# A dilated GraphSAGE behind masked attention: output parts of two batches held until each batch norm, the last products in all eight PSUM banks, and tiles of the first loads given other homes

## The chip, the cores and the metric

The kernel runs on one core of one Trainium2 chip. The metric is the device time of one execution in microseconds (us), the median of a few runs. The profile is one more execution, recorded by the hardware profiler. Its spans are named by engine: PE (TensorE matmul), PEld (its weight load), DVE (VectorE), ACT (ScalarE), POOL (GpSimd) and SP (SyncE, which here only issues DMAs).

## The reference, cut to what matters

Sixteen graphs (b) of 1024 nodes and 128 features go through two residual layers. The first is attention with eight heads, masked and weighted by the adjacency matrix. The second first thins the adjacency row by row ("dilation"), and then runs three SAGE convolutions, each with a batch norm over all graphs and nodes:

```python
h = jnp.maximum(_layernorm(x), 0.0)
x = x + attention(h, adj, ...)                  # mask adj == 0, softmax, times adj
h = jnp.maximum(_layernorm(x), 0.0)
adj_d = _dilate(adj, mask)                      # sequential in the rows of each graph
def _sage(x, adj, Wr, Wx, b, mf):
    agg = einsum('bij,bjd->bid', adj, x) / deg
    out = agg @ Wr + x @ Wx + b
    return out / maximum(norm(out), 1e-12) * mf[..., None]
def _bn(x, g, b):
    m, v = mean(x, axis=(0, 1)), var(x, axis=(0, 1))
    return (x - m) * rsqrt(v + 1e-5) * g + b
h1 = _bn(relu(_sage(h,  adj_d, Wr1, Wx1, b1, mf)), g1, be1)
h2 = _bn(relu(_sage(h1, adj_d, Wr2, Wx2, b2, mf)), g2, be2)
h3 = _bn(relu(_sage(h2, adj_d, Wr3, Wx3, b3, mf)), g3, be3)
x = x + (concatenate([h1, h2, h3]) * mf @ Wl + bl) * mf
```

Each batch norm needs the whole of its layer before anything of the next layer can start.

## The kernel before, in words

Everything is in one function, `swept` (L35); `walked` (L1327) is a fallback behind a flag and is not taken here.

**First part, 0 to about 2370 us.** `attention()` (L462) goes over `turns` of (graph b, half c of 512 nodes, block m of 128 nodes). A turn has two halves g of four heads. For each half PE makes scores in `scores` (L521): sixteen 32x32 matmuls add minus infinity where there is no edge (L536, from `nomask`), four products of keys and queries follow (L542). ACT takes the exponential (L579), DVE multiplies by the adjacency (L584), PE sums (`values`, L466). `turn_over` (L479) makes a turn's transposed adjacency: PE transposes (L487), ACT copies (L490) and makes `nomask` (L494), and six DMAs on SP's queue copy `nomask` onto itself at other partitions (L498, L499). `prepare(b)` (L282) makes keys, queries and values; its layer norm ends in a power on POOL (L272). `dilation()` (L621) runs beside attention; for its first block it reads 16 adjacency rows tiles of 512 KB (L650, POOL's queue). `biases()` (L90) splits five bias vectors in three bf16 pieces. `node_masks()` (L227) makes the mask columns.

**The three SAGE layers, about 2370 to 3498 us.** A turn is (layer L, graph b, half c), about 10 us. `nodes` (L1083) is a generator: PE makes the node's own part (L1094) and 4 x 16 aggregation products (L1108, "sums"); then, one turn later and between the next turn's sums, "scaled" (DVE L1126, ACT square L1131), "norm" (DVE L1134 to ACT L1137), "result" (DVE L1139 to L1141), "transposed" (PE L1145, ACT copy into `hTs` L1146) and "end" (DVE statistics, L1148). DVE also masks the next turn's adjacency (L142). `given` (L1074) makes the next graph's products with Wr, `incoming` (L1066) applies the batch norm to a graph on ACT (L1072). `output_part(L-1, b, h, ...)` (L1018) is what a layer adds to the output: four matmuls (L1023) and four DVE adds into `prev` (L1030), with a store to DRAM after the second half. It runs beside the turn c = 1 of graph b, except for the last graph, whose two parts come after the layer.

**After each layer** (L1281 to L1294): the last half's stages without anything beside them, the matmuls of the last graph's parts, the aggregate of the statistics (L1285), the square root on ACT (L1288), four small DVE steps to the scale and shift (`affine`, L1289 to L1292), then the DVE adds of the parts. Then ACT applies `affine` to the next layer's graph 0.

**The last products, about 3498 us to the end.** For each graph `come` (L1305) applies the batch norm on ACT (two instructions), `output_part(2, ...)` makes two halves in three PSUM banks in turn ("y", "n", "o", L1317). Half 0 takes four DVE adds. In half 1 DVE adds two blocks, ACT multiplies the other two (L1038) and DVE adds those in one step (L1039). SP stores each half to `out` (L1041).

**What sets the order.** PE, ACT and DVE keep the order in which the Python code calls them (`manual_schedule`, L1183). SP and POOL issue in an order that the framework chooses by when a tile's buffer is free. A tile belongs to a tag of its pool with so many buffers, and a new tile waits until the tag's oldest tile is no longer read. A DMA also waits for the one issued eight before it on the same kind of queue. Readers of one PSUM tile on different engines are put one after the other, in the order of the code.

## Time and profile before

| | us |
|---|---|
| median of 3 runs (3560.0 to 3562.39) | 3561.78 |
| the profiled execution | 3556.3 |
| its span, first to last instruction | 3554.4 |
| PE busy | 3445.8 (97%) |
| DVE busy | 3174.0 (89%) |
| ACT busy | 2290.9 (64%) |
| start of the first exponential, L579 | 27.73 |
| end of `affine` of the three layers, L1292 | 2763.2, 3133.2, 3498.6 |
| end of the last DVE add, L1039 | 3547.2 |

Busy is a sum over instructions. The span also holds what comes before and behind them on their engines, and the execution has 1.9 us around the span. A row of the timeline gives the start in us, the busy time in us, engine, line, operation, output<-input with shapes, the count, and in brackets the idle time of that engine just before and what ended it. A row of stretches gives the busy time of each engine in it, the granted TensorE clock (PEclk, 1.00 is full), the mean busy share of the DMA engines and what they moved.

### The profile page before, as it was taken

The page shows a single profiled execution, that of the slowest core. Times are in us where ns is not written, and L with a number is a line of the kernel's source. Part 1 is how long each engine was busy: PE and PEld are TensorE (multiplying, and loading weights), DVE is VectorE, ACT ScalarE, POOL GpSimd, SP SyncE. Part 2 cuts the span into 40 slices and gives each one's busy share as a digit, 9 for nine tenths or more (in the row PEclk, how much of TensorE's full clock was granted, in tenths as well). Part 3 has the DMA queues.
Part 4 walks back from the last instruction along what each step waited for, and adds up shares of the span by engine and source line. Part 5 has one row for each costly group of instructions (what it writes and reads, how often), then busy time and mean ns, then how long its engine had stood idle before and what let it go on. Part 6 is the DMA issues. An engine that isn't in the chain of part 4 may idle for free.

```text
span 3554.4 us, 86070 instructions
## 1 busy us (share of the span) xinstructions
PE 3445.8 (97%) x34855; PEld 1893.8 (53%) x34855; DVE 3174.0 (89%) x5254; ACT 2290.9 (64%) x3781; POOL 179.0 (5%) x253
## 2 busy tenths in 40 slices
PE   8999999999999999999999999999999899999997
PEld 3333333333333333333333333338999899989996
DVE  7999999999989999999999999987878788878886
ACT  6699689679769869968976885873232333322224
POOL 2000000000000000000000000000000000000000
PEclk9999999999999999999999999999999999999999
DMA  7356356447537636735754763667999799989995
GB/s 231 102 169 201 123 159 199 142 135 214 168 111 222 195 116 201 227 111 170 235 157 133 235 205 110 209 213 285 331 331 326 266 328 328 329 295 333 333 332 184
DMA packets 650122, 772.27 MB, mean 217 GB/s; under 512 B 173264, under 2 KB 569168, under 8 KB 637424
## 3 DMA queue, kind: packets, MB, share of 16 engines
q1 hardware_dynamic: 632672, 708.58, 61.7%
q0 software_dynamic: 15456, 57.30, 4.9%
q8 instruction: 275, 4.51, 0.5%
q14 instruction: 135, 1.11, 0.1%
q10 hardware_dynamic: 1584, 0.79, 0.1%
HBM read 508.50 MB, written 157.29 MB: 187 GB/s over the span
## 4 chain that ended last, share of the span: by engine, by line
PE 48%; DVE 39%; ACT 6%; DMA 3%; issue 3%; SPq 1%; POOL 0%; ACTq 0%; DVEq 0%; POOLq 0%
DVE w L584 16%; PE pg L1108 16%; PE sc L542 6%; PE acc L469 5%; PE acc L474 5%; DVE wr L872 4%; PE pn L1079 2%; DVE hit L807 2%; ACT e L579 2%; PE sc L536 2%; PE own L1094 2%; PE py L1023 2%; DMA nomask<-nomask 1%; PE pt L1145 1%; DVE aT L142 1%
## 5 line engine op out<-in xcount | busy, mean ns | idle before, releaser
L584 DVE TENSOR_TENSOR w<-e,aT 128x1024 f32<-128x1024 f32 x1024 | 1204.2, 1217 | 91.2 <-ACT e L579 90.9
L579 ACT ACTIVATE e<-sc 128x1024 f32<-128x1024 f32 x1024 | 990.9, 1020 | 376.1 <-PE sc L542 375.0
L1108 PE MATMUL pg<-y,aT 128*128 128x128 f32 (+1 forms) x6144 | 738.0, 275 | 0.0
L1108 PEld LDWEIGHTS pg<-y,aT 128*128 128x128 f32 x6144 | 712.4, 192 | 0.0
L469 PE MATMUL acc<-w,v_both 128*32 128x512 f32 x4096 | 673.1, 607 | 8.6 <-DVE w L584 3.8
L474 PE MATMUL acc<-e,eps 128*32 128x512 f32 x4096 | 650.5, 596 | 0.0
L542 PE MATMUL sc<-qT,kT 32*128 32x512 f32 x4096 | 584.8, 641 | 0.0
L142 DVE SCALAR_TENSOR_TENSOR aT<-mr,aT 128x1024 f32<-128x1024 bf16 x384 | 458.9, 1217 | 0.0
L474 PEld LDWEIGHTS acc<-e,eps 128*32 128x32 f32 x4096 | 165.9, 110 | 295.1 <-issue 285.2
L1131 ACT ACTIVATE sq<-o 128x512 f32<-128x512 f32 x96 | 60.5, 631 | 363.4 <-DVE o L1126 363.4
L872 DVE TENSOR_TENSOR_SCAN wr<-rk 128x1024 f16<-128x1024 bf16 x128 | 291.7, 2279 | 0.0
L536 PEld LDWEIGHTS <-never 32*32 32x32 bf16 x8192 | 79.1, 88 | 345.3 <-issue 323.6
L536 PE MATMUL sc<-nomask,never 32*32 32x512 bf16 x8192 | 249.6, 385 | 12.5 <-ACT e L579 8.0
L469 PEld LDWEIGHTS acc<-w,v_both 128*32 128x32 f32 x4096 | 106.4, 108 | 233.9 <-DVE w L584 140.2
L542 PEld LDWEIGHTS sc<-qT,kT 32*128 32x128 f32 x4096 | 160.1, 183 | 116.6 <-issue 116.6
L487 PEld LDWEIGHTS pa<-ident,a 128*128 128x128 f32 x1024 | 108.2, 142 | 182.4 <-issue 143.5
L1146 ACT COPY hT<-pt 128x512 f32<-128x512 f32 x96 | 56.3, 587 | 224.2 <-PE pt L1145 223.2
L1126 DVE SCALAR_TENSOR_TENSOR o<-pg,rdeg,mine 128x128 f32<-128x128 f32 x384 | 108.1, 344 | 92.2 <-PE pg L1108 90.4
L885 ACT ACTIVATE wr<-wr,th 128x1024 f16<-128x1024 f16 x128 | 148.0, 1156 | 46.7 <-DVE wr L872 45.8
L487 PE MATMUL pa<-ident,a 128*128 128x128 f32 x1024 | 168.7, 288 | 7.0 <-DMA a<-in_adj 6.3
L494 ACT ACTIVATE nomask<-aT 128x512 bf16<-128x512 f32 x256 | 161.4, 630 | 8.1
L490 ACT COPY aT<-pa 128x512 f32<-128x512 f32 x256 | 151.6, 592 | 11.5 <-PE pa L487 6.8
(222 smaller groups left out, 3949.8 us busy)
## 6 DMA issues: line engine op xcount, KB each, us to landing
aT<-aT_d SPq DMA_DIRECT2D x94, 2048.0 KB, 9.0
mr<-mr_d SPq DMA_DIRECT2D x188, 512.0 KB, 5.8
aT_d<-aT SPq DMA_DIRECT2D x256, 256.0 KB, 4.0
a<-in_adj SPq DMA_DIRECT2D x253, 256.0 KB, 4.0
ad<-in_adj SPq DMA_DIRECT2D x112, 512.0 KB, 4.1
nomask<-nomask SPq DMA_DIRECT2D x512, 96.0 KB, 2.7
nomask<-nomask SPq DMA_DIRECT2D x512, 64.0 KB, 2.6
nomask<-nomask SPq DMA_DIRECT2D x512, 32.0 KB, 2.6
```

Of the source, the lines that this page charges most:

```text
L142: nc.vector.scalar_tensor_tensor(part, mrs[h][:, j : j + 2, :].rearrange("p j n -> p (j n)"), 0.0, part, ALU.is_equal, ALU.mult)
L469: nc.tensor.matmul(acc[g][32 * j : 32 * j + 32, :], v1[:, m, 2 * j + g, :], ws[j // 2][:, j % 2, :], start=(m == 0), stop=False,)
L474: nc.tensor.matmul(acc[g][32 * j : 32 * j + 32, :], eps8, es[j // 2][:, j % 2, :], start=False, stop=(m == NB - 1),)
L487: nc.tensor.transpose(pa[:, k * P : (k + 1) * P], a[:, k, :], ident)
L490: nc.scalar.copy(aT[:, 0, :], pa)
L494: nc.scalar.activation(nomask[:, 0, :], aT[:, 0, :], AF.Relu, bias=1.0, scale=-1e38, accum_out=zeros[:, i : i + 1])
L536: nc.tensor.matmul(scs[j // 2][to : to + 32, j % 2, :], never[rows, rows], nomask[rows, j, :], start=True, stop=False, tile_position=(32 * ...
L542: nc.tensor.matmul(scs[j // 2][:, j % 2, :], kT[rows, mm], qTs[c][rows, g, :], start=False, stop=True, tile_position=(32 * j, 0),)
L579: nc.scalar.activation(e, scs[q], AF.Exp, scale=1.0 / math.sqrt(HD))
L584: nc.vector.tensor_tensor(w, es[q], aT.to_broadcast([P, 2, HN]), ALU.mult)
L872: nc.vector.tensor_tensor_scan(wrs[b], rk(b, 1, N + 1), rk(b, 2, N + 2), -1023.0, ALU.add, ALU.add)
L1108: nc.tensor.matmul(pg[:, i // 2, at : at + width], aT[:, j, i * P : (i + 1) * P], y[:, j, :width], start=(j == 0), stop=(j == NB - 1),)
```

## The change

1. **First loads.** `biases()` starts ahead of the loads of x. Its three pieces become three tiles, one in tag "mr" and two in tag "xin", the home of the x tiles. The node mask and its float copy move to tag "ad", the home of the dilation's row tiles. `node_masks()` is called in the first half of turn 2 instead of turn 0. The six loads of the batch norm's weights (`norms`) move from a constant tile to a tile that is opened after the first part.
2. **Held parts.** In layers 1 and 2 the output parts of the last two graphs are held: the matmuls of graph 14 stand right behind the last half's "scaled", those of graph 15 behind its "end", in banks "o", "g", "g", "y" ("g" is half of a two-bank score tile). All 16 DVE adds come after `affine`.
3. **The step to `affine`.** For the last half of a layer the statistics are taken before ACT's copy. One small DVE step is put beside the square root, and one goes.
4. **Last products.** Each graph has two banks, in a rotation over all eight: two score tiles, then "t" and "n", then "o" and "y". PE makes both halves of a graph at once, `come` runs two graphs ahead, and the add of ACT's two blocks is made after the next graph's first four adds.

The parts of the diff that carry this:

```diff
         for i, name in enumerate(names):
             nc.gpsimd.dma_start(vecs[0][:, i, :], t[name].rearrange("(o d) -> o d", o=1))
+        pieces = [
+            shared.tile([1, n, D], BF, name=f"pieces{i}", tag="xin" if i else "mr", bufs=3 if i else 4)
+            for i in range(3)
+        ]
         yield
-        pieces = shared.tile([1, 3, n, D], BF, name="pieces", tag="mr", bufs=4)
...
+        bias_pieces = biases()
+        next(bias_pieces)
         load_x(0)
         for i in range(3):
             load(i, nc.scalar)
-        bias_pieces = biases()
-        next(bias_pieces)
...
-        nr_i = pool.tile([B * NB, P], I32, name="nr_i", tag="qT")
+        nr_i = shared.tile([B * NB, P], I32, name="nr_i", tag="ad", bufs=2)
...
                     elif g == 0:
+                        go_on_with(True)
+                    if (i, g) == (2, 0):
                         node_masks()
-                        go_on_with(True)
...
+        last_half = b == B - 1 and c == 1
+        if last_half:
+            nc.vector.bn_stats(late["stats"][:, 2 * b + c, :], pt)
         nc.scalar.copy(hTs[b][:, c * HN : (c + 1) * HN], pt)
         yield "transposed"
-        nc.vector.bn_stats(late["stats"][:, 2 * b + c, :], pt)
+        if not last_half:
+            nc.vector.bn_stats(late["stats"][:, 2 * b + c, :], pt)
...
+            held, last_parts = ["o", "g", "g", "y"], []
...
                     if c == 1 and L > 0:
-                        parts = [output_part(L - 1, b, h, hT, prev, "y" if more or h == 0 else "o") for h in range(2)]
-                        if more:
+                        at_end = b + 2 >= B
+                        parts = [output_part(L - 1, b, h, hT, prev, held.pop(0) if at_end else "y") for h in range(2)]
+                        if at_end:
+                            last_parts += parts
+                        else:
...
-            go(before, "scaled", "norm", "result", "transposed", "end")
-            for part in parts:
+            go(before, "scaled")
+            for part in last_parts[:2]:
                 next(part)
+            go(before, "norm", "result", "transposed", "end")
+            for part in last_parts[2:]:
+                next(part)
...
             nc.scalar.activation(mv[:, 1:2], mv[:, 1:2], AF.Sqrt, bias=bn_eps)
+            nc.vector.scalar_tensor_tensor(mv[:, 2:3], mv[:, 0:1], -1.0, late["norms"][:, L, 0:1], ALU.mult, ALU.mult)
             nc.vector.reciprocal(mv[:, 1:2], mv[:, 1:2])
-            nc.vector.tensor_tensor(affine[:, 0:1], norms[:, L, 0:1], mv[:, 1:2], ALU.mult)
-            nc.vector.tensor_tensor(mv[:, 0:1], mv[:, 0:1], affine[:, 0:1], ALU.mult)
-            nc.vector.tensor_tensor(affine[:, 1:2], norms[:, L, 1:2], mv[:, 0:1], ALU.subtract)
-            for part in parts:
+            nc.vector.tensor_tensor(affine[:, 0:1], late["norms"][:, L, 0:1], mv[:, 1:2], ALU.mult)
+            nc.vector.scalar_tensor_tensor(
+                affine[:, 1:2], mv[:, 2:3], mv[:, 1:2], late["norms"][:, L, 1:2], ALU.mult, ALU.add
+            )
+            for part in last_parts:
                 whole(part)
...
+        def products(b):
+            if b % 4 < 2:
+                both = ps_s.tile([P, 2, 512], F32, name=f"py_3_{b}", tag="sc")
+                pys = [both[:, c, :] for c in range(2)]
+            else:
+                pys = [bank(f"py_3_{b}_{c}", ("t", "n", "o", "y")[2 * (b % 2) + c]) for c in range(2)]
...
+        come(0)
+        come(1)
+        before = None
+        for b in range(B):
+            pys = products(b)
+            of = [pys[k // HB][:, (k % HB) * P : (k % HB + 1) * P] for k in range(NB)]
+            for k in range(HB):
+                add(b, k, of[k])
+            leave(b, 0)
+            if before:
+                finish(*before)
+            tmp = late["pool"].tile([P, NB - mine, D], F32, name=f"tmp_{b}", tag="mine")
+            for k in range(mine, NB):
+                nc.scalar.mul(tmp[:, k - mine, :], of[k], mf2[:, b * NB + k : b * NB + k + 1])
+            for k in range(HB, mine):
+                add(b, k, of[k])
+            come(b + 2)
+            before = b, tmp
+        finish(*before)
```

`add` is one DVE multiply-and-add of a 128x128 block, `finish` one DVE add of two blocks from `tmp` and the store of half 1, `leave` the store of a half (`mine` is 6).

## The prediction

> **What bounds the kernel now.** I read the page's chain that ended last first, then the places that the change touches in the timeline: the first 35 us, a layer's end, the tail. The chain's first lines:

> ```profile
> PE 48%; DVE 39%; ACT 6%; DMA 3%; issue 3%; SPq 1%; POOL 0%; ACTq 0%; DVEq 0%; POOLq 0%
> ```

> Most of the time goes along PE and DVE, in loops that are not touched. So the change can only work on dead time at three kinds of places. The start:

> ```profile
> 9.34 1.35 SPq L653 DMA_DIRECT2D ad<-in_adj  x1
> ...
> 10.32 1.06 POOL L272 TENSOR_TENSOR rs_a<-rs_a,minus_half 128x4 f32<-128x4 f32 x1
> ...
> 12.38 0.62 SPq L498 DMA_DIRECT2D nomask<-nomask  x1
> ...
> 24.42 1.25 PE L536 MATMUL sc<-nomask,never 32*32 32x512 bf16 x6 [0.32 <-DMA nomask<-nomask]
> ...
> 27.73 1.94 ACT L579 ACTIVATE e<-sc 128x1024 f32<-128x1024 f32 x2 [4.68 <-PE sc L542]
> ```

> POOL's power starts at 10.32, though DVE had its input ready at 7.92 (L271, 7.75 for 0.17): six loads of batch norm weights stand ahead of it. The first nomask copy is issued at 12.38, though ACT had the mask at 8.67: two x loads and two ad loads stand ahead on SP. PE waits for these copies until 24.42.

> The end of layer 2 (graph 15's last aggregate ends at 3124.2), with the clock in stretches of 1 us:

> ```profile
> 3128.55 1.09 PE L1145 MATMUL pt<-ident,o 128*128 128x128 f32 x4 [4.33 <-DVE o L1141]
> 3129.22 3.54 PEld L1023 LDWEIGHTS py<-weights,h 128*128 128x128 f32 x16
> ...
> 3130.30 0.70 DVE L1148 BATCH_NORM_STATS2 stats<-pt 128x6 f32<-128x512 f32 x1 [1.89 <-ACT hT L1146]
> ```
> ```profile
> 3126.00:3127.00 1.00, 0.00 (x0) 0.00 (x0) 0.82 (x2) 0.11 (x1) 0.00 (x0) 1.00 0.80 248
> 3127.00:3128.00 1.00, 0.00 (x0) 0.00 (x0) 0.66 (x4) 0.20 (x1) 0.00 (x0) 0.81 1.04 410
> 3128.00:3129.00 1.00, 0.45 (x2) 0.48 (x3) 0.41 (x1) 0.00 (x0) 0.00 (x0) 0.50 1.03 426
> ```

> PE sits idle 4.33 us, the granted clock halves, and the statistics wait for ACT's copy. The tail, one graph of sixteen:

> ```profile
> 3508.59 1.64 DVE L1030 SCALAR_TENSOR_TENSOR outs<-py,mf,outs 128x128 f32<-128x128 f32 x6
> ...
> 3510.32 0.63 ACT L1038 ACTIVATE tmp<-py,mf 128x128 f32<-128x128 f32 x2 [0.45 <-DVE outs L1030]
> 3510.97 0.43 DVE L1039 TENSOR_TENSOR outs<-outs,tmp 128x256 f32<-128x256 f32 x1 [0.75 <-ACT tmp L1038]
> ```

> DVE and ACT take turns: 1.64 + 0.09 + 0.63 + 0.02 + 0.35 to the next graph's adds make the period of 2.73 us.

> **The start: 5.5 us saved.** In the program of the change POOL's power waits for DVE alone: 7.95 in place of 10.32, so h follows at about 9.25, not 11.61. PE is just done with the weights' transposes by then (10.03). The chain h, hT, pa, aT, pk, pq keeps its lengths (11.61 to 20.04, less 2.36), so q is written by ACT at 17.7 to 19.2. On SP the x loads now wait for the pieces' copies and the ad loads for the node mask, so they stand behind. The first nomask copy can go at about 8.9, the sixth at about 12. With 2.6 us to land (page, copies' median) to 5.4 (the same in the first 75 us) all are there at 15 to 17.5, before PE is done with pq (17.7). Then 16 mask matmuls (1.7, from four in 0.43) and 2.09 for L542: the first exponential at 21.5 in place of 27.73, 6.2 us. What is late next: ACT, which from 30.6 on is busy without a gap; it simply runs ahead by that much.

> What this costs: xt 1 is issued only when a_4 and the bias copies have landed (6 to 6.9 us by the DMA view), about 20.3, and lands at about 26. Its statistics on DVE are due then, behind the first w, and the next w waits for an exponential that ends at 28, so I book 0; without that cover it is 1 us. `node_masks` in turn 2 puts 0.22 on DVE, a PE transpose behind the sums of the previous turn and 0.8 on DVE behind that, about 1.7 with the wait, ahead of w at 47.06; but DVE next waited 1.60 there for an ad load (51.09). Booked 0.2; at turn 0 it had cost 0.6, which goes. The stretch 40 to 60 moves 335 to 348 GB/s with the DMA engines full; one of the two ad loads (0.5 MB, 1.5 us) now falls into it: booked 0.7. So 6.2 - 0.7 = 5.5, ends 2.5 (DMA takes the lead back) and 6.7. The six weight loads, 0.55 each on POOL, go to about 2375, where POOL waits 3 to 5 us between issues and its next loads wait for PE anyway: 0.

> **The step to affine: 2.4 us.** At each of three layer ends the statistics no longer wait for ACT's copy (0.59 + 0.03), and the copy runs beside the aggregate (1.02): -0.62. One of four DVE steps of 0.195 goes, and the new one (0.16) fits into DVE's 0.36 wait for the square root: -0.19. Together 3 x 0.81. If readers were not put in this order it is 3 x 0.19.

> **Graph 14's parts: 3.6 us.** Beside its turn they take two times 0.89 us of PE (L1023 on the chain), with PE the bound. Now 16 matmuls run in the idle 4.33 us. PE then still comes to pt after DVE's o (6.1 against 5.3 us into the turn), so no wait opens: 2 x 1.8. No pg waits for a DMA in this stage, so the loads have slack; lower end 2 x 1.2. The eight adds (2.2 us of DVE) move behind `affine`, ahead of the masks of the next turn: these end at about 9 us after affine, and PE needs them at 16. Held banks are free after 1.1 to 4.4 us; own needs "o" at 5, pg at 5 to 8. Booked 0. The queue behind: POOL's store of graph 14 and load of the next `prev`, wanted 20 us later.

> **The clock: 3.7 us.** No row shows PE warm after a gap of about 2.3 us, so I bound it. From below: the three gaps of the page (clock down 3.3 to 5 us after the last matmul) with nothing gained if any gap cools it, 0. [...] pt takes 0.63 in place of 1.09 at both ends (2 x 0.46); parts of graph 15 fill the next gap; and layer 3's first products (3134.06 to 3141.22, 7.16 us, all at 0.50) take 1.06 + 0.67 + 1.06 + 0.3 + 1.1 = 4.2 and some issue: -2.8. By the rows alone the term is 0 to 3.7[...]. I take 3.7, since the rows do have drops only after 3.2 us. At layer 1's end PE stays idle 4.7 us, and nothing changes.

> **The tail: 6.5 us.** ACT's two blocks no longer stand between DVE's adds and DVE's last step. Graphs in two-bank tiles: ACT waits for four adds (1.10), then 0.09 + 0.63, 0.03, two adds 0.55, so 2.40, with `finish` (0.43) inside the wait. Graphs in single banks: ACT does not wait, and ACT's own 0.63 + 1.52 sets 2.15 to 2.2. The mean is 2.29, so 16 x 2.29 + 0.45 = 37.1. Ahead of it DVE now has 16 adds, 4.4 (3.3 from affine to the first out add before). So affine to last add is 41.5, against 3547.2 - 3498.6 = 48.7: 7.2. The first products wait for "g" (2.3 us after affine); at half clock 16 take 3.6 and DVE starts 1.5 later; I take half of that. SP waits for the loads of graphs 14 and 15 before most stores, until 8.5 us after affine (7.9 before), and 0.52 MB per 2.29 us is 229 GB/s, with the DMA engines at 0.69 for 205 now: just covered. Ends 4.5 and 7.3.

> Sum: 5.5 + 2.4 + 3.6 + 3.7 + 6.5 = 21.7. The profiled execution, 3556.3, would become 3534.6. The runs' median lies 5.5 above it; the same step gives 3540.

> **Rivals.**
> - Clock still drops: 3.7 and 0.7 of the tail go: 3544. For it: [...] after 4.3 us of work at half clock it stayed at half. Chance 0.22.
> - The loads lead again in 40 to 60 us: 3 us of the start go, 3543. For it: two waits of DVE for ad there, 4.2 in total. Chance 0.15.
> - The tail stays in lockstep or at the stores' rate (2.6 or more per graph): 3545. Against: no store is on the chain but one. Chance 0.08.
> - Slower: SP is held by x load 1, which waits for the bias copies. Behind it stand the masks of turn 2, needed by PE at about 37. They need 11 us, so a landing after 26 us costs one for one; a loss of 7 net of 21.7 needs it at 55. The slowest copy now lands at about 23.7. Chance 0.02.
> - The banks or homes do nothing at all (a place where another wait takes over each gain): within 0.2%, 0.03.
> - My forecast, 3540: 0.50.

> **How the numbers follow.** A measurement can tell about 0.2%, 7.1 us. All cases but the last two are faster: 0.95; same 0.03; slower 0.02. With all upper ends 24.6 and a spread of 2 it is 3535; with start 2.5, clock 0 and tail 4.5 together 3549, and 2 for the spread. I say 3534 to 3551.

> **What would show it.** First exponential near 21.5; first nomask copy near 9; statistics right behind pt; affine steps 0.58 apart in place of 0.77; PEclk 1.00 at pt and through layer 3's first products; tail period 2.2 to 2.4 with ACT nearly full; end of the last add 41 to 43 us after affine. Wrong if DVE or ACT waits for DMA between 25 and 60, if pt still takes 1.09, or if SP's stores lag behind DVE.

## The result, and the profile after

| | before | after |
|---|---|---|
| median of five runs, us | 3561.08 | 3540.96 |
| lowest and highest | 3558.74, 3562.39 | 3538.31, 3553.21 |
| the profiled execution | 3556.3 | 3540.29 |

The ratio of the runs is 0.995, with a 95% interval of 0.9932 to 0.9967: 20 us faster, known to some 6 us either way. The pair of profiled executions differs by 16.0 us only. That gap of four is itself a subject below, since everything that is read by stage comes from single traces. The layers are counted 1 to 3 here, as in the prediction (L = 0 to 2 in the code).

Where the two traces part, stage by stage (start times unless the row says end):

| | before | after | gained on the way here |
|---|---|---|---|
| first exponential | 27.73 | 20.14 | 7.6 |
| 65th product w (exponential times adjacency, DVE L584, L594 after) | 172.55 | 169.68 | -4.7 |
| first aggregate of layer 1 | 2417.26 | 2416.82 | -2.4 |
| affine of layer 2, end | 3133.16 | 3128.30 | 4.4 |
| first aggregate of layer 3 | 3141.22 | 3133.44 | 2.9 |
| affine of layer 3, end | 3498.61 | 3487.64 | 3.2 |
| last DVE add, end | 3547.25 | 3529.66 | 6.6 |
| end of the span | 3554.41 | 3538.50 | -1.7 |

The chain that ended last is of no use here. On the page of the profile after it holds nothing but the last DVE steps ("DVE 0%"); two of the last three stores have no landing in this trace, which is probably why it stops there. So the reading goes by place. The start, from the timeline of after (start, busy, engine, line, operation, tiles, count, and in brackets the idle time before with what ended it):

```profile
7.53 1.04 POOL L274 TENSOR_TENSOR rs_a<-rs_a,minus_half 128x4 f32<-128x4 f32 x1 [2.39 <-DVE rs_a L273]
...
9.07 0.62 SPq L507 DMA_DIRECT2D nomask<-nomask  x1
...
17.15 0.65 PE L545 MATMUL sc<-nomask,never 32*32 32x512 bf16 x16
...
20.14 1.92 ACT L589 ACTIVATE e<-sc 128x1024 f32<-128x1024 f32 x2
```

POOL's power waits for DVE alone and stands at 7.53, the first nomask copy at 9.07. All sixteen mask matmuls run in one piece of 0.65 with no wait for a DMA, and the first exponential is 7.6 us earlier, more than the 6.2 forecast. What is late next, in DVE's own timeline of after:

```profile
21.18 2.36 DVE L594 TENSOR_TENSOR w<-e,aT 128x1024 f32<-128x1024 f32 x2 [4.99 <-ACT e L589]
27.43 0.49 DVE L266 BATCH_NORM_STATS2 st_a<-xt 128x6 f32<-128x128 f32 x2 [3.89 <-DMA xt<-in_x]
...
41.81 0.29 DVE L674 SCALAR_TENSOR_TENSOR rk<-ad,nothing 128x128 bf16<-128x128 f32 x1 [1.20 <-DMA ad<-in_adj]
...
43.69 0.29 DVE L234 COPY mf<-mps 128x128 f32<-128x128 f32 x1 [0.42 <-PE mps L233]
...
51.24 0.29 DVE L674 SCALAR_TENSOR_TENSOR rk<-ad,nothing 128x128 bf16<-128x128 f32 x1 [0.96 <-DMA ad<-in_adj]
```

The statistics of x tile 1 wait 3.89 us: the tile is issued at 20.73, behind the bias copies, and they stand between the first w and the next. (A wait on an earlier DMA of the queues shows in before, too: the ninth DMA of SP and ACT, bk at 6.18, stood 2.7 us until the first had landed.) At 41.81 and 51.24 DVE waits for dilation loads as before. At 43.69 the mask columns cost 1.3 us, of which 0.42 is a wait for PE. Of the lead of 8.2 us at the first w, 2.85 are left at 80 us.

The end of layer 2 in after (pt is the transposes of the last half, py graph 15's held parts, pg the aggregates):

```profile
3124.58 1.09 PE L1143 MATMUL pt<-ident,o 128*128 128x128 f32 x4 [2.54 <-DVE o L1139]
...
3125.46 3.11 PE L1033 MATMUL py<-weights,h 128*128 128x128 f32 x16
3125.70 0.70 DVE L1146 BATCH_NORM_STATS2 stats<-pt 128x6 f32<-128x512 f32 x1 [1.27 <-PE pt L1143]
...
3128.09 0.21 DVE L1303 SCALAR_TENSOR_TENSOR affine<-mv,norms 128x1 f32<-128x1 f32 x1
...
3133.44 5.52 PE L1106 MATMUL pg<-y,aT 128*128 128x128 f32 x48
```

The statistics stand right behind pt (0.03 us; ACT's copy is no longer between), and affine is complete 8.06 us after the last aggregate, where it took 8.93. But pt still takes 1.09: the clock fell (0.50 from 3124.45 to 3127.87). It was back by the first products of layer 3 (3129.21), and affine to the first aggregate took 5.14 us in place of 8.06. The first aggregate in before:

```profile
3141.22 5.56 PE L1108 MATMUL pg<-y,aT 128*128 128x128 f32 x48
```

At the end of layer 3 in after the same gap left the clock up:

```profile
3484.38 0.63 PE L1143 MATMUL pt<-ident,o 128*128 128x128 f32 x4 [2.55 <-DVE o L1139]
```

There pt takes 0.63 (1.09 in before), and the clock falls later, at 3489.68.

The tail in after:

```profile
3489.86 5.35 PE L1335 MATMUL py<-weights,h 128*128 128x128 f32 x32 [3.07 <-DVE acc L1038]
...
3493.46 1.13 DVE L1343 SCALAR_TENSOR_TENSOR outs<-py,mf,outs 128x128 f32<-128x128 f32 x4 [1.68 <-PE py L1335]
...
3508.09 0.62 ACT L1372 ACTIVATE tmp<-py,mf 128x128 f32<-128x128 f32 x2
3508.38 0.42 DVE L1356 TENSOR_TENSOR outs<-outs,tmp 128x256 f32<-128x256 f32 x1
...
3508.74 1.65 DVE L1343 SCALAR_TENSOR_TENSOR outs<-py,mf,outs 128x128 f32<-128x128 f32 x6
```

ACT's multiply (3508.09) now runs beside DVE's adds; no row of this graph has a wait. Four graphs take 9.05 us, 2.26 each against 2.73. The first add starts 5.8 us after affine, because PE waited 3.07 for banks that the held adds occupied and then ran its first products at half clock (0.50 from 3489.68 to 3493.09). The end is worse than before. SP's stores in after, then in before (the start of the first issue, the time to the end of the last, how many):

```profile
3519.46 11.19 SPq L1349 DMA_DIRECT2D out<-outs  x11
```
```profile
3530.56 17.09 SPq L1041 DMA_DIRECT2D out<-outs  x13
```

The last issue ends at 3530.65, which is 0.99 behind the last add; in before at 3547.65, 0.40 behind it. SP's wait for the last landings ends 5.33 us behind the last add, against 3.79. The stores had been "just covered", and at the end three of them stand together.

### The profile page after: what moved, and what is told of

Read it like the earlier page. It is cut to its first block, busy times and chain, and to the rows that moved or that the text cites. A ratio compares the mean times of both kernels' runs of the same rounds, so it can differ in the third digit from the quotient of the medians.

```text
span 3538.5 us, 86073 instructions
## 1 busy us (share of the span) xinstructions
PE 3433.7 (97%) x34855; PEld 1884.6 (53%) x34855; DVE 3172.6 (90%) x5254; ACT 2289.3 (65%) x3781; POOL 177.6 (5%) x253
## 5 line engine op out<-in xcount | busy, mean ns | idle before, releaser
L594 DVE TENSOR_TENSOR w<-e,aT 128x1024 f32<-128x1024 f32 x1024 | 1203.7, 1217 | 98.0 <-ACT e L589 97.6
L545 PE MATMUL sc<-nomask,never 32*32 32x512 bf16 x8192 | 247.0, 385 | 10.8 <-ACT e L589 7.5
```

Of the source, the lines that this page charges most:

```text
L545: nc.tensor.matmul(scs[j // 2][to : to + 32, j % 2, :], never[rows, rows], nomask[rows, j, :], start=True, stop=False, tile_position=(32 * ...
L594: nc.vector.tensor_tensor(w, es[q], aT.to_broadcast([P, 2, HN]), ALU.mult)
```

## Experiments

Each run's time stands beside the kernel before on the same chip, whose medians in the three sets of runs were 3561.58, 3558.55 and 3559.01. Single executions of it went from 3554.4 to 3568.0.

### Part 1 alone, and everything but part 1

The first is the kernel before with part 1 of the diff above, the second is the change with part 1 taken out again:

```diff
-        load_x(0)
-        for i in range(3):
-            load(i, nc.scalar)
         bias_pieces = biases()
         next(bias_pieces)
+        load_x(0)
+        for i in range(3):
+            load(i, nc.scalar)
...
-                        node_masks()
                         go_on_with(True)
+                    if (i, g) == (2, 0):
+                        node_masks()
```

> The kernel before with part 1 of the change alone. The prediction's term (5.5 us of the start reach the end): 3555.5. Theory A, from the trace of after, in which DVE waits 3.9 us for x tile 1 and again ahead of the masks of turn 2, so that 2.85 of the 7.6 us are left at 80 us and 0.4 at the end of attention: first exponential at about 20, a lead of 2.9 us at 80 us over before, 0 to 3 at the first aggregate, and a median of 3558 to 3561. Theory B, that the lead is lost to the loads of the dilation at random and 2.9 is the rule: 3558.

Measured: 3557.05, ratio 0.9989 (0.9981 to 0.9997), so 4.0 us, between 1 and 7, which leaves the prediction's 5.5 and both theories open. The first exponential is at 20.46, the lead at 170 us 2.36. In this trace, however, the first aggregate of layer 1 is at 2423.84, 6.6 us later than in before.

> The change without its part 1. By the prediction's term 3541 + 5.5 = 3546.5; by theory A 3541 to 3544, with the first exponential back at 27.7 and the stages from 2370 us on as long as in the change, affine to affine 366.4 and 359.3 us.

Measured: 3550.78, ratio 0.9969 (0.9958 to 0.9981), slower than either theory gave. By these medians part 1 is worth 4.0 us in the one run and, as 20.1 less 10.8, 9.3 in the other. First exponential 28.65. The layers are as long as in the change: affine to affine 366.3 and 359.4. Its trace, too, lost time in the first part: it is 0.6 us behind before at 170 us and 10.2 at the first aggregate of layer 1.

Neither run can be read by one trace. For each block of 16 of the 1024 products w, I took its length minus the shortest that any of the fourteen traces has, and added these up from the 65th product to the last: before 3.8, after 6.3, start_alone 12.8, start_undone 13.3, the other ten 3.6 to 10.4. Most of the losses sit at a few places (about 320, 573 to 640, 906 and 1206 us). There DVE waits for dilation's loads (L686 or L696 of the two kernels, "rk<-rk,gl", 1.4 us in all in before, 7.6 in start_undone) and PE for nomask copies. The sum is no smaller with part 1 than without: 8.0 on average of the three traces without (before, before_again, start_undone), 8.3 of the nine with it unchanged. So what part 1 is worth is read ahead of them, at the 65th product: 172.6, 175.3 and 173.2 without, 166.2 to 170.2 with (mean of nine 168.2). That is 5.4 us, and the forecast was 5.5.

### Is it the moved matmuls that keep the clock?

In gap_idle, graph 14's held parts issue no matmuls and DVE adds graph 15's products twice:

```diff
-        py = bank(f"py_{L}_{b}_{c}", tag).rearrange("p (k d) -> p k d", d=D)
-        for i in range(HB):
...
+        if b == B - 2:
+            yield
+            py = lent[c]
+        else:
+            py = bank(f"py_{L}_{b}_{c}", tag).rearrange("p (k d) -> p k d", d=D)
+            lent[c] = py
```

> The change with graph 14's 16 output matmuls in layers 1 and 2 left out, so that its output parts are not computed (DVE adds graph 15's products in their place, so its work stays); nothing is put into the gap behind the last aggregate. It tells the clock from the moved matmuls. If the busy gap keeps the clock (the prediction's term of 3.7): the granted clock falls at both ends, the first products of layer 3 take about 7 us in place of 5.1 behind affine, pt takes 1.09 at both, 3544.5. If the fall depends on something else: affine to first aggregate stays 5.1 and the time 3541.

Measured: 3541.44, ratio 0.9947 (0.9933 to 0.996), the time of the change. Affine to first aggregate of layer 3 is 5.27, affine to the last add even 40.24. For the 2.9 us the second theory holds: filling the gap with these matmuls is not what brought them. At layer 3's pt the first one holds: with the gap left at 4.33 us pt takes 1.09, and 0.63 in after. (Graph 14's parts are not computed in it.)

> The change with only graph 15's parts held, graph 14's beside its turn as before. By the prediction's terms 3.6 for graph 14's parts and 3.7 for the clock it loses 7.3: 3548. If the clock has another cause it loses only the matmuls: 3544.5. If the parts had been hidden beside the turn: no more than gap_idle loses.

```diff
-            held, last_parts = ["o", "g", "g", "y"], []
+            held, last_parts = ["y", "o"], []
...
-                        at_end = b + 2 >= B
+                        at_end = b + 1 >= B
...
-            go(before, "scaled")
-            for part in last_parts[:2]:
-                next(part)
-            go(before, "norm", "result", "transposed", "end")
-            for part in last_parts[2:]:
+            go(before, "scaled", "norm", "result", "transposed", "end")
+            for part in last_parts:
                 next(part)
```

Measured: 3545.61, ratio 0.9956 (0.9942 to 0.9969). From affine of layer 1 to the last add it takes 771.0 us, against 767.7 in after and 768.1 in gap_idle. So moving graph 14's matmuls is worth about 3 us net. Layer 3 alone shows 1.8 (first to last aggregate 348.4 against 346.6), exactly the two times 0.89 that the prediction had. But what is left of it in the end comes from layer 2: from layer 3's first aggregate to the last add last_graph_only takes 396.1 us and after 396.2, because the held adds stand in the tail.

### Where the clock falls

In before the falls of the granted clock start at 980.65, 1881.76, 2144.59, 2188.96, 2431.31, 2758.99, 3127.63 and 3492.86, each a whole number of 3.413 us from the others, and each lasts one, three or four such stretches. (One more, at 3547.47, stands behind PE's last work.) In after they start at 977.47, 2144.83, 2431.55, 2755.82, 3124.45 and 3489.68, again whole numbers of 3.413 us apart, and last one or four stretches; counted from each trace's start, the grid of after stands 0.24 us behind that of before. Laid on this grid, the end of layer 2 in before reads (busy time of PE, PEld, DVE, ACT, POOL, then PEclk, DMA share, GB/s):

```profile
3124.22:3127.63 3.41, 0.00 (x1) 0.00 (x0) 2.27 (x8) 0.83 (x2) 0.00 (x0) 1.00 1.03 345
3127.63:3131.04 3.41, 2.49 (x12) 2.52 (x13) 1.45 (x4) 0.59 (x1) 0.00 (x0) 0.50 0.93 384
3131.04:3134.45 3.41, 2.41 (x12) 2.11 (x12) 2.94 (x11) 1.55 (x3) 0.00 (x0) 0.50 0.09 38
```

The stretch with PE idle (0.00 of 3.41 us) is followed by half clock (PEclk 0.50). In the next two PE is busy for 2.49 and 2.41 of 3.41 us, and the clock stays down. The same program once more, and the change once more:

> The kernel before once more, for its trace. If the fall of the clock behind layer 2 is set by where the grid of 3.4 us stands: a fall of 1 to 4 stretches, affine to first aggregate 5.1 to 8.1. If it is fixed by the program: 4 stretches and 8.06 again. The stalls from 300 to 2200 us fall elsewhere than in the first trace.

> The change once more, for its trace. By the grid: a fall of 0 to 2 stretches at layers 2 and 3, pt at 0.63 or 1.09 by where it stands, affine to last add 40 to 42. By the program: 1 and 1, 5.14 and 42.0 again.

Measured: 3558.99 and 3538.26, one execution each. The end of layer 2 in before_again:

```profile
3130.33:3133.74 3.41, 0.00 (x0) 0.00 (x0) 2.28 (x9) 0.83 (x2) 0.00 (x0) 1.00 1.12 387
3133.74:3137.16 3.42, 2.78 (x13) 2.81 (x14) 1.50 (x3) 0.58 (x1) 0.00 (x0) 0.50 0.83 340
3137.16:3140.57 3.41, 1.64 (x15) 1.45 (x14) 2.95 (x12) 1.81 (x3) 0.00 (x0) 1.00 0.10 38
```

The gap stands 0.3 us otherwise on the grid (PE stops at 3130.05, the stretch begins at 3130.33; in before both are at 3124.22). The stretch at half clock now holds 2.78 us of work, and the clock comes back after one stretch: affine to first aggregate 5.14, without any part of the change. In start_alone, which has before's layer ends, it is 5.14 as well. So before has 8.06, 5.14 and 5.14, and the first was the one that I had. In the change:

```profile
3121.04:3124.46 3.42, 0.99 (x9) 0.80 (x8) 2.26 (x7) 0.84 (x2) 0.00 (x0) 1.00 0.95 331
3124.46:3127.87 3.41, 3.29 (x16) 3.33 (x17) 1.93 (x4) 0.88 (x2) 0.00 (x0) 0.50 0.85 317
3127.87:3131.28 3.41, 2.09 (x16) 1.71 (x16) 3.38 (x15) 2.11 (x3) 0.54 (x1) 1.00 0.14 58
```

0.99 us of work in a stretch, 29%, did not prevent the fall. It lasts one stretch, and pt and graph 15's matmuls make up 3.29 us of that one. After_again gave 5.14 and, at layer 3, 42.01 from affine to the last add, as in after. That is the expectation "by the program", not "by the grid". One reason can be read: at the end of layer 1 the first aggregate starts 0.25 to 0.27 us after the clock's return in both traces of after (2769.47 to 2769.74, 2766.98 to 2767.23), so in both the work that follows stands at the same place on the grid. In early_both below it starts 1.5 us ahead of the return, and there the same gap left pt fast at layer 2 (0.63) and slow at layer 3 (1.09), the reverse of after, with the same layer ends in the program: here where the gap stands on the grid decided. And gap_idle at the end of layer 2:

```profile
3118.44:3121.85 3.41, 0.96 (x9) 0.77 (x7) 1.65 (x5) 0.63 (x1) 0.00 (x0) 1.00 1.00 313
3121.85:3125.27 3.42, 1.54 (x8) 1.57 (x9) 1.78 (x6) 0.20 (x1) 0.00 (x0) 0.50 0.98 407
3125.27:3128.68 3.41, 3.28 (x15) 2.98 (x15) 3.14 (x12) 2.06 (x4) 0.00 (x0) 0.50 0.27 111
```

Here two stretches were slow and the first aggregate still came 5.27 us after affine. At the three layer ends of before and of after the clock fell behind stretches in which PE was busy for a share of 0.00 to 0.31, and not behind those with 0.54 and more; in before_again a stretch with 0.48 (1.64 us, above) was not followed by a fall. It came back behind stretches with 0.95 to 1.00, behind 0.81 in before_again, and stayed down behind 0.01 to 0.80; in other traces three stretches with 0.84, 0.86 and 1.00 did not bring it back. These shares were measured at the layer ends alone. At the start of layer 1 the clock fell behind 0.47 in before and 0.59 in after, and in the first part of these two behind 0.74 to 0.78, though other stretches with 0.76 did not bring it down. What else counts is open. By the 3.413 us a gap of 4.33 leaves at least 2.17 us of idle time in one stretch wherever it stands, and one of 2.54 at least 1.27; that is an estimate from the lengths alone. With the remaining gap of 2.54 the clock fell at layer 2 in all six traces with the change's layer 2; at layer 3 the same gap brought it down in one of the six.

> The change with extra matmuls, whose result nobody reads, in the gaps of PE at all three layer ends: 32 and 20 at the end of layer 1, 14 and 10 at layer 2, 14 and 12 at layer 3, so that no stretch of 3.4 us is left mostly idle. If the granted clock falls because a stretch of the fixed grid was mostly idle: no fall at any of the three ends, affine to first aggregate 5.1 at both (now 7.8 and 5.1), pt 0.63 at all three, together 3 to 4 us off the sum of the stages. If the fall has another cause: the same falls, and the time 3541 or a little more where the extra matmuls stand in the way.

```diff
+    def warm(L, n, hT):
+        if n:
+            pw = bank(f"pw_{L}_{n}", "n")
+            for i in range(n):
+                nc.tensor.matmul(pw[:, :P], hT[:, :P], wts[f"Wr{L + 1}"], start=True, stop=True)
...
             for part in last_parts[:2]:
                 next(part)
+            warm(L, 14 if L else 32, hT)
             go(before, "norm", "result", "transposed", "end")
             for part in last_parts[2:]:
                 next(part)
+            warm(L, (20, 10, 12)[L], hT)
```

Measured: 3541.96, ratio 0.9949 (0.9936 to 0.9963). No fall at any layer end, but 32 of these matmuls take 7.31 us and push pt from 4.7 to 7.0 us behind the last aggregate. What the clock gave, the extra work took. With half as many:

```diff
-            warm(L, 14 if L else 32, hT)
+            warm(L, 7 if L else 16, hT)
...
-            warm(L, (20, 10, 12)[L], hT)
+            warm(L, (10, 4, 9)[L], hT)
```

> As warm_ends, with about half the extra matmuls (16 and 10, 7 and 4, 7 and 9), since there 32 took 7.3 us and pushed pt back by 2 us. If a mostly idle stretch of the grid is the cause of the fall: no fall, last aggregate to affine 8.0 at layer 1 and 7.6 at layers 2 and 3, affine to first aggregate 5.1 to 5.3 at both, affine to last add about 40.3; 4 to 5 us off the sum of the stages against the change. If not, the times of the change: 8.5, 8.1 and 7.6; 7.8 and 5.1; 42.0.

Measured: 3533.06, ratio 0.9923 (0.9909 to 0.9937), the lowest of all medians; its interval just overlaps that of the change. From the last aggregate of layer 1 to the last add it takes 772.7 us, against 776.2 and 775.8 in the two traces of the change: 3.3 us, less than the 4 to 5 expected. The end of layer 2 on the grid:

```profile
3115.82:3119.24 3.42, 2.44 (x23) 2.27 (x22) 2.20 (x7) 0.44 (x2) 0.00 (x0) 1.00 0.93 321
3119.24:3122.65 3.41, 2.55 (x23) 2.36 (x22) 3.17 (x13) 2.17 (x4) 0.00 (x0) 1.00 0.50 211
```

No stretch is below 0.7, and the clock is full. Layer 2 ends 7.60 us after its last aggregate (8.06), the tail takes 40.47 (42.01). At layer 1 one stretch with 1.43 us of work was left and one fall, so affine to first aggregate took 6.69 there (7.82 in after, 5.14 without any fall in all_three). So here the idle gap did cost clock, and the change filled it only in part.

### The tail, its adds, and the start once more

> The change with the last products of before (three banks in turn, ACT's blocks inside the same half). The prediction's term for the tail is 6.5 net: 3547.5, and affine to the last add about 49 to 51 us in place of 42.0 (48.7 in before, and now with eight more adds ahead of it). If the tail of before had been hidden behind its stores or loads: no change, 3541.

Measured: 3550.67, ratio 0.9979 (0.9972 to 0.9985); the edit is part 4 of the change, reversed:

```diff
-        def products(b):
...
-            if before:
-                finish(*before)
...
+            for c in range(2):
+                parts.append(output_part(2, b, c, hT, prev, ("y", "n", "o")[(2 * b + c) % 3]))
+                next(parts[-1])
+                if c == 0:
+                    come(b + 1)
+                if len(parts) > 1:
+                    whole(parts.pop(0))
```

Affine to the last add is 51.8, and 7.6 from there to the end of the span: 9.8 us more ahead of the last add, 1.3 less behind it. The tail was not hidden. The net of 8.5 is more than the pair's 4.9, because here graph 14's held adds stand ahead of the old tail, too (48.6 in before).

> The change with six of graph 14's eight DVE adds moved ahead of affine, into DVE's waits (two behind the last half's aggregate, four in the wait for pt). If the held parts of graph 14 give nothing at the end of layer 3, because their adds stand ahead of the last products: affine to last add falls by 1 to 1.6 us at the end (42.0 now), with the step from the last aggregate to affine not longer by more than 0.2. If the last products wait for ACT and PE alone: no change.

```diff
+            for part in last_parts[:1] * 2:
+                next(part)
-            go(before, "norm", "result", "transposed", "end")
+            go(before, "norm", "result")
+            for part in last_parts[:1] * 2 + last_parts[1:2] * 2:
+                next(part)
+            go(before, "transposed", "end")
```

(each `next` now makes one add of graph 14.) Measured: 3541.68, ratio 0.9954 (0.994 to 0.9968): the time of the change, as far as runs can tell. Its trace lost 10.4 us by the sum of blocks in the first part, so the stage is read:

```profile
3484.22 0.60 DVE L1038 SCALAR_TENSOR_TENSOR acc<-py,mf,acc 128x128 f32<-128x128 f32 x2
...
3487.25 1.12 DVE L1038 SCALAR_TENSOR_TENSOR acc<-py,mf,acc 128x128 f32<-128x128 f32 x4
...
3494.74 1.13 DVE L1350 SCALAR_TENSOR_TENSOR outs<-py,mf,outs 128x128 f32<-128x128 f32 x4 [1.28 <-PE py L1342]
```

Two adds stand behind the aggregate's scaling, four in the wait for pt, and the last aggregate to affine takes 7.73 (7.60). The first add of the tail comes 3.9 us after affine (5.8), affine to the last add 40.17 (42.01). So graph 14's adds do stand in the way of the tail, by 1.8 us, as much as holding its matmuls gained in layer 3.

> The change with the second bias piece back in the home mr, so that x tile 1 can be loaded before the bias copies have landed, and with the mask columns made in turn 0 again. If these two are what eats the lead (DVE's waits of 3.9 us for x tile 1 and about 2 ahead of the masks): statistics of x tile 1 near 23.5 in place of 27.4 and a lead over the change of 2 to 4 us at 80 us, 3537 to 3539. If the loads of the dilation set the pace from 40 to 60 us in any case: a lead of 0 to 1 at 80 us and the time unchanged.

```diff
-            shared.tile([1, n, D], BF, name=f"pieces{i}", tag="xin" if i else "mr", bufs=3 if i else 4)
+            shared.tile([1, n, D], BF, name=f"pieces{i}", tag="xin" if i > 1 else "mr", bufs=3 if i > 1 else 4)
...
-                    if (i, g) == (2, 0):
+                    if (i, g) == (0, 0):
                         node_masks()
```

Measured: 3537.2, ratio 0.9944 (0.993 to 0.9958). The wait for x tile 1 is gone (its statistics are at 25.89, not near 23.5), but the first w comes at 23.62, since the mask columns now wait 6.45 us for PE. At 170 us the lead over after is 3.3 us, over the mean of the nine traces 1.9, inside their own spread. Undecided.

> The change with the extra matmuls of warm_less, the adds of adds_early, the second bias piece in mr and the mask columns in turn 0 ahead of the work that held them up in early_both. If the three causes are independent: start 4 to 6 us (early_both had 3.3 at 170 us, and its first w is at 23.6 where 21.2 can be), clock 4 to 5, adds 0 to 1 beside the clock: 3530 to 3533. If the loads of 40 to 60 us hold the start back: 3534.

The edits of warm_less, adds_early and early_both together, except that the mask columns stand ahead of the step that held them up:

```diff
                     elif g == 0:
+                        node_masks()
                         go_on_with(True)
-                    if (i, g) == (2, 0):
-                        node_masks()
```

Measured: 3534.6, ratio 0.9925 (0.9912 to 0.9939). Clock and adds came: from the last aggregate of layer 1 to the last add 770.1. The start did not; its timeline:

```profile
35.40 0.29 DVE L673 SCALAR_TENSOR_TENSOR rk<-ad,nothing 128x128 bf16<-128x128 f32 x1 [2.06 <-DMA ad<-in_adj]
...
38.88 0.62 PE L545 MATMUL sc<-nomask,never 32*32 32x512 bf16 x4 [3.07 <-DMA nomask<-nomask]
...
43.77 1.94 ACT L588 ACTIVATE e<-sc 128x1024 f32<-128x1024 f32 x2 [5.13 <-PE sc L551]
...
44.82 2.36 DVE L593 TENSOR_TENSOR w<-e,aT 128x1024 f32<-128x1024 f32 x2 [3.76 <-ACT e L588]
```

With everything earlier, DVE waits 2.06 for a dilation load at 35.40 and PE 3.07 for a nomask copy at 38.88. From 35 to 40 us PE is busy for 1.44 of 5 us, the clock falls for two stretches, and the exponential waits 5.13. The DMA engines are at 1.03 to 1.09 from 30 to 45 us. The lead over after at 170 us is -1.2. So in this trace the loads of the first 60 us do set a limit, and moving the rest further ahead only changed who waits.

## Why the prediction was right, point by point

- **The sum**, 21.7 against 20.1 in the medians: inside the range, and the forecast is off by 1 us. Part of that is luck: the clock was put too high and the end of the tail left out. The terms as the traces have them (5.4, 2.4, 3.6, about 1.4, 4.9) add up to 17.7, well inside the 12 to 24 of the runs' interval.
- **The start, 5.5**: 5.4 at 170 us. The two parts of it were off in opposite ways. The first exponential gained 7.6, not 6.2. The step "Its statistics on DVE are due then [...] so I book 0; without that cover it is 1 us" failed: the cover was gone, x tile 1 could be used at 27.4, not 26, and DVE waited 3.9 us (2.8 in after_again, 2.5 in warm_less).
- **The step to affine, 2.4**: 0.68, 0.87 and 0.87 in the pair, 2.4 without the clock at pt. No run isolates it, but at layer 2 the step takes 8.93 in all three traces with before's end and 8.05 or 8.06 in five of the six with the change's (7.60 in early_both, whose pt was fast).
- **Graph 14's parts, 3.6**: the turns gained 1.8 each. Layer 2 shows 2.5 in the pair, but before also began it with 1.4 us at half clock, worth 0.7 (early_both began it with 1.5 us of that and took 0.73 longer than after). Their adds, "booked 0" at layer 2, cost 1.8 in the tail, so that nothing of layer 3's 1.8 is left in the end; the tail's sum had them in its 16 adds.
- **The clock, 3.7**: in the pair 2.9 and 0.46, so the number fits, and the step failed. It was an estimate of mine: no row of before has PE at full clock behind a gap of 2.3 us. That pt takes 0.63 in place of 1.09 at both ends was wrong at layer 2, where most was booked: the clock fell there in all six traces (in after at 3124.45, with pt at 1.09). At layer 3's pt it came true in five of the six. The clock fell there, too, but later (3489.68 in after), while PE waited 3.07 us for banks. At the end of layer 2 the fall in before came 3.41 us behind the last aggregate (3124.22 to 3127.63), and in after a stretch that was idle for 71% was enough. The 2.9 us were there, too, in two of the three traces with before's layer ends. What the change owns is 0.46 at layer 3's pt, and at layer 2 that the fall was short in all six traces of it. Against one long fall in three that is a mean of 1 us, and with the 0.46 about 1.4; it is argued from three traces and not shown. The rival "Clock still drops" was right about layer 2.
- **The tail, 6.5**: 6.6 to the last add (period 2.26 for 2.29, 42.0 for 42.2). The 1.7 behind it, stores that no longer keep up, were not in the sum; "just covered" was right for the period and wrong for the end.
- **The range**: the upper ends as stated (6.7, 2.4, 3.6, 3.7 and 7.3) add up to 23.7, not 24.6, which would have put its low end near 3536.
- **The median's 5.5 us above the profiled execution** was carried over unchanged. After's profiled execution lay on its median. Before's had the fewest stalls of the three traces without part 1, so the pair shows 16.0 where the runs show 20.1.

What stays open: why the loads of dilation come late at some of the few places in one execution and not in another, and with that how much of a single trace's 6 us in the first part belongs to any edit.

## What to carry to other kernels

A lead won at the start is worth what it still is behind the first stretch in which the DMA engines are full; read it there, over several traces, and not at the first instruction (here 7.6 us at the first exponential and 5.4 at the 65th product, with the DMA engines at 0.94 to 1.04 from 20 to 60 us in after). A clock that falls in one trace is not a constant of the program (affine to first aggregate took 8.06 and 5.14 us in two traces of before): lay PE's busy time on the trace's own grid before crediting an edit with it, and then fill the gap itself, with work counted so that it ends ahead of the instruction it must not delay (32 matmuls in 7.31 us pushed pt from 4.7 to 7.0). If work is held back until a barrier, its other half (here the adds) comes due behind the barrier and should go into waits ahead of it (six adds, 1.8 us of the tail in adds_early).
